# Plain products instead of seven-product ones for the first two query graphs, and another place for a small fold

## The chip, the cores and the metric

The kernel runs on one core of a Trainium2 chip. The metric is the device time of one execution in microseconds (us). Engines are named as in the profile: PE is TensorE, DVE is VectorE, ACT is ScalarE, POOL is GpSimd, SP is the engine that issues the DMAs.

## What is computed

Sixteen graphs of 1024 nodes with 256 channels share one adjacency matrix. Each batch element goes through a graph-weighted attention with a layer norm, and then through two graph convolutions with a layer norm. Cut to what matters:

```python
fea = transpose(x)                                  # B, C, N
c_adj = mean(fea, axis=1)
diff = c_adj[:, None, :] - c_adj[:, :, None]
A = abs(abs(sigmoid(diff) - 0.5) - 0.5) * 2
Wg = adj[None] * (A + A^T) * 0.5
q = relu(einsum('bcn,bnm->bcm', fea, Wg) * para)    # the query graph
k, v = x @ kv_w
x1 = layernorm(x + softmax(q k^T * scale) v)        # 4 heads of 64
h = relu(x1 w1_loop + adj (x1 w1_neigh) + b1)
h = relu(h w2_loop + adj (h w2_neigh) + b2)
out = layernorm(x1 + (x1 + h) * 0.5)
```

The change touches how the query graph q is made: a product of x^T (256 x 1024) with the weighted adjacency matrix Wg (1024 x 1024), different for each batch element.

## The kernel before

All arithmetic is in fp32. A "row" is a tile of 128 x 1024; 21 of them circulate in SBUF and are given out again as their last readers finish. PSUM is divided into three "big" tiles of two banks and two "bank" tiles of one.

The order of all work is written out by hand in `run()`; each engine executes its instructions in that order and waits by semaphores. For each batch element the order is: four attention units (`att.scores(u)`, `att.outputs(u)`; a unit is a pair of heads and half of the nodes), between which the graph convolution of the element before it (`conv.first`, `second`, `last`) is placed; then the query graph of the next element; then its keys and values. `att.add(u)` divides by the softmax denominators (a small PE product with the constant `fold`, L477), adds to x (L487) and sums (L488). `BlockedNorm` is the layer norm after the attention: `mean()` folds these sums on PE (`fold_sums`, L214) and subtracts (L265, L268); `squares()` squares on ACT (L274) and sums on DVE (L275); `variance()` folds again (L214) and takes the power on POOL (L281); `scale()` and `spread()` finish it.

The query graph of an element is prepared in 128-row parts t = 0 to 7. `load(t)` brings a part of adj (L343), `likeness(t)` makes the weight on ACT with Abs and Tanh (L348, L349), `times_adj(t)` multiplies by adj on DVE (L354). From these parts, seven block products in the manner of Strassen and Winograd are made in place of eight: `left` forms four sums of blocks of x on POOL (L361 to L364), `right(k)` four differences of weights on DVE for the parts k and 4 + k (L374 to L377), `step(k)` the seven products on PE (L402), accumulated over k = 0 to 3 in seven PSUM banks (three big tiles and one bank tile), and `end` combines them on DVE with seven additions (L411 to L418), multiplies by `para` (L420) and applies Relu (L421).

Element 0 is special: its query graph comes first of all, beside the loads of all constants. During element 0, when no graph convolution runs yet (`conv` is None), the transposed adjacency matrix is made as well: `adj_blocked(mt)` loads it in 128-byte pieces into rows (L165), `turn_adj` transposes them on DVE (L694). The query graph of element 1 is made in that stretch. From element 2 on every period has the same order.

The helper classes that the change touches are `Queries` (L324 to L422), its callers in `run()` (L669 to L709 for element 0; `second`, L730 to L735; L742 to L763; L767 to L798), and the path L834 to L852, which is executed only where a denominator is out of range and isn't executed here.

Of the kernel before, what the change touches and what calls it, by code (L numbers as in the profile page):

```python
# [18 lines left out]
def kernel(  # L19
# [63 lines left out]
    def big_psum(name):  # L83
        return psum.tile([P, N], F32, tag="big", name=name, bufs=3)
# [239 lines left out]
    class Queries:  # L324

# [5 lines left out]


        def __init__(self, b, xb):
            self.b, self.xb = b, xb
            self.wg, self.adj, self.T, self.T4 = {}, {}, {}, {}

        def load(self, t):
            self.adj[t] = row_tile(f"adj_{self.b}_{t}")
            nc.sync.dma_start(out=self.adj[t], in_=adj[t * P:(t + 1) * P, :])  # L343

        def likeness(self, t):

            wg = row_tile(f"wg_{self.b}_{t}")
            nc.scalar.activation(wg, self.c_row, AF.Abs, bias=self.c_col[:, t:t + 1], scale=-1.0)  # L348
            nc.scalar.activation(wg, wg, AF.Tanh, scale=-0.5)  # L349
            self.wg[t] = wg  # L350

        def times_adj(self, t):
            wg = self.wg[t]
            nc.vector.scalar_tensor_tensor(wg, wg, 1.0, self.adj.pop(t), op0=ALU.add, op1=ALU.mult)  # L354

        def block(self, i, j):
            return self.xb[:, j * TJ:(j + 1) * TJ, ts(i, P)]
# [19 lines left out]
            nc.vector.tensor_sub(t4, hi[:, h0], t12[:, h1])  # L377
            self.T[k] = (t12, t4)

        def weigh(self, k):  # L380
            for t in (k, TJ + k):
                self.load(t)
                self.likeness(t)
                self.times_adj(t)
            self.right(k)

        def step(self, k):
            if k == 0:
                a, b, c = (big_psum(f"g_ps_{self.b}_{i}") for i in range(3))
                h0, h1 = ts(0, FB), ts(1, FB)  # L390
                self.p = {1: a[:, h0], 6: a[:, h1], 7: b[:, h0], 5: b[:, h1], 2: c[:, h0], 3: c[:, h1],
                          4: bank_psum(f"g_ps_{self.b}_3")}
                self.a = a
            lo, hi = self.wg.pop(k), self.wg.pop(TJ + k)
            t12, t4 = self.T.pop(k)
            h0, h1 = ts(0, FB), ts(1, FB)
            terms = {1: (self.block(0, 0), lo[:, h0]), 2: (self.block(0, 1), hi[:, h0]), 3: (self.S[3], hi[:, h1]),
                     4: (self.block(1, 1), t4), 5: (self.S[0], t12[:, h0]), 6: (self.S[1], t12[:, h1]),
                     7: (self.S[2], lo[:, h1])}
            for n in (1, 6, 2, 7, 4, 5, 3):  # L400
                x_n, w_n = terms[n]
                nc.tensor.matmul(self.p[n], x_n[:, k, :], w_n, start=(k == 0), stop=(k == TJ - 1))  # L402

# [258 lines left out]
    def run():  # L662

        xT, c_col = prepare_first(x_first)  # L669
        q = Queries(0, x_first)  # L670
        q.left(nc.gpsimd)
        for k in range(TJ):
            q.load(k)
            q.load(TJ + k)
        load_para()
        blocked = load_blocked(1, "1")
        load_weights()

        def first_weights():
            q.c_row, q.c_col = first_row(c_col), c_col  # L680
            q.likeness(0)

        kT = keys(0, xT, first_weights)
        q.likeness(TJ)
        q.times_adj(0)
        v = values(0, xT, nc.vector.tensor_copy)
        q.times_adj(TJ)
        q.right(0)
        xb = load_x(1, "1")
        tiles = {}  # L690

        def turn_adj(mts):
            for mt in mts:
                nc.vector.transpose(adjT_sb[:, mt, :], tiles.pop(mt))  # L694

        ready = {}
        for k in range(1, TJ):
            for t in (k, TJ + k):
                q.likeness(t)
                q.times_adj(t)  # L700
            q.right(k)
        for k in range(TJ):
            q.step(k)
            if k == 1:
                xB = load_blocked(0, "a0")
                ready["xT"], ready["part"] = prepare(blocked, "1")
            if k == 2:
                ready["mean"] = means(ready["part"], "1")
        qT = q.end()  # L709
        old = conv = None  # L710
        for b in range(B):
            more = b + 1 < B
            att = Attention(b, xB, qT, kT, v)
            if conv and more:
                xb = load_x(b + 1, str(b + 1))

            def first():
                blocked = load_blocked(b + 1, str(b + 1))
                conv.first(blocks=True)
                if old:  # L720
                    old.moments()
                conv.turn_blocks(0)
                ready["xT"], ready["part"] = prepare(blocked, str(b + 1))
                if old:
                    old.finish(out[b - 2])
                conv.turn_blocks(1)
                att.add(0)
                ready["mean"] = means(ready["part"], str(b + 1))

            def second():  # L730
                q.c_row, q.c_col = ready["mean"]
                q.left(nc.gpsimd)
                q.weigh(0)
                conv.second(blocks=True)
                att.add(1)  # L735

            def last():
                conv.last()
                att.add(2)

            between = [first, second, last] if conv and more else []
            if more:  # L742
                q = Queries(b + 1, xb)
            for u in range(len(UNITS)):
                att.scores(u)
                if u == 3 and more:
                    for t in (2, TJ + 2, 3, TJ + 3):
                        q.load(t)
                    for t in (2, TJ + 2, 3, TJ + 3):
                        q.likeness(t)  # L750
                    q.right(1)
                if u and not between:
                    att.add(u - 1)
                att.outputs(u)
                if u == 2 and more:
                    if not conv:
                        q.c_row, q.c_col = ready["mean"]
                        q.left(nc.gpsimd)
                        q.weigh(0)
                    for t in (1, TJ + 1):  # L760
                        q.load(t)
                        q.likeness(t)
                        q.times_adj(t)  # L763
                if u < 3 and between:
                    between[u]()
            norm = BlockedNorm(xB, att.sums, str(b))
            if more:  # L767
                xT = ready["xT"]
                if not conv:
                    for mt in range(4):  # L770
                        tiles[mt] = adj_blocked(mt)

                def pair(k):
                    q.times_adj(k)
                    q.times_adj(TJ + k)
                    q.right(k)

                pair(2)
                q.step(0)
                att.add(3)  # L780
                pair(3)
                q.step(1)
                if not conv:
                    turn_adj(range(4))
                    for mt in range(4, NT):
                        tiles[mt] = adj_blocked(mt)
                norm.mean()
                norm.squares()
                q.step(2)
                q.step(3)  # L790
                qT = q.end()
                xB = load_blocked(b + 1, f"a{b + 1}")
                kT = keys(b + 1, xT, norm.variance)
                norm.scale()
                norm.spread()
                if not conv:
                    turn_adj(range(4, NT))
                v = values(b + 1, xT)  # L798
            else:
                conv.first(lambda: att.add(3))  # L800
                norm.mean()
                norm.squares()
                conv.turn(1)
                conv.neighbours(0)
                norm.variance()
                conv.neighbours(1)
                norm.scale()
                norm.spread()
                conv.last()
                for k, c in ((b - 2, old), (b - 1, conv)):  # L810
                    c.moments()
                    c.finish(out[k])
            old, conv = conv, GraphConv(b, norm.x1, norm.x1T)
        conv.first()
        conv.second()
        conv.ending(out[B - 1])
# [17 lines left out]
    with tc.If(count < P):  # L834
        with tc.For_i(0, B, 1) as b:
# [2 lines left out]
            q = Queries("z", xb)  # L838
            q.c_row, q.c_col = means(part, "z")
            kT, v = keys("z", xT), values("z", xT)  # L840
            q.left(nc.vector)
            for k in range(TJ):
                q.weigh(k)
                q.step(k)
            safe_attention("z", xb, q.end(), kT, v)
            layernorm(xb, "za")
            conv = GraphConv("z", xb, channel_major(blocked_of(xb, "z"), "x1T_z"))
# [34 lines left out]
```

## Time and profile before

| what | value |
|---|---|
| time, median of 3 runs | 2290.58 us (2290.38 to 2290.88) |
| profiled execution, span | 2288.2 us (that run: 2289.93 us) |
| granted PE clock, mean | 0.994 |
| PE products of the query graph (L402) | 896 records, 0.6 us each as shown, 0.43 us from start to start |
| weighted part on ACT (L348 + L349) | 1152 + 1058 ns |
| times adj on DVE (L354) | 1206 ns |
| a difference of weights on DVE (L374 to L377) | 684 to 693 ns |
| an addition at the end (L412 to L418) | 678 to 687 ns |
| times para (L420), Relu (L421) | 1221 ns, 1057 ns |

An fp32 product of 128 x 512 appears as two records of matmul. Records overlap, so the distance from start to start tells what one costs PE. In the lists of waits a row reads: who waited, for whom, us in total, how often, the longest. In a timeline a row reads: start, length, engine, line, operation, tiles, shape, number of instructions, and in brackets the idle time before it and what ended it.

### The profile page before, as it was taken

The page shows a single profiled execution, that of the slowest core. Times are in us where ns is not written, and L with a number is a line of the kernel's source. Part 1 is how long each engine was busy: PE and PEld are TensorE (multiplying, and loading weights), DVE is VectorE, ACT ScalarE, POOL GpSimd, SP SyncE. Part 2 cuts the span into 40 slices and gives each one's busy share as a digit, 9 for nine tenths or more (in the row PEclk, how much of TensorE's full clock was granted, in tenths as well). Part 3 has the DMA queues.
Part 4 walks back from the last instruction along what each step waited for, and adds up shares of the span by engine and source line. Part 5 has one row for each costly group of instructions (what it writes and reads, how often), then busy time and mean ns, then how long its engine had stood idle before and what let it go on. Part 6 is the DMA issues. An engine that isn't in the chain of part 4 may idle for free.

```text
span 2288.2 us, 22626 instructions
## 1 busy us (share of the span) xinstructions
PE 2230.9 (97%) x8294; PEld 1066.4 (47%) x8294; DVE 1806.1 (79%) x2423; ACT 946.4 (41%) x1028; POOL 200.1 (9%) x112
## 2 busy tenths in 40 slices
PE   7989999999999999999999999999999999999997
PEld 4334454444544445454444544445444454444454
DVE  6887878878688797887978778887887968879855
ACT  4633534434354343444344344353443535434420
POOL 1100020010200102001020100102001020010001
PEclk9999999999999999999999999999999999999998
DMA  7195252353423425243261522625235342343102
GB/s 186 37 129 111 60 89 73 66 119 74 83 74 70 115 65 107 78 79 83 60 129 56 92 74 55 129 64 88 70 69 116 74 92 67 75 108 65 37 14 80
DMA packets 568470, 189.39 MB, mean 83 GB/s; under 512 B 487072, under 2 KB 551456, under 8 KB 568352
## 3 DMA queue, kind: packets, MB, share of 16 engines
q1 hardware_dynamic: 568080, 187.35, 38.3%
q8 instruction: 67, 1.10, 0.2%
q14 instruction: 51, 0.42, 0.1%
q10 hardware_dynamic: 272, 0.52, 0.1%
HBM read 146.93 MB, written 40.89 MB: 82 GB/s over the span
## 4 chain that ended last, share of the span: by engine, by line
PE 77%; DVE 20%; issue 1%; DMA 1%; SPq 0%; ACT 0%; DVEq 0%; POOLq 0%; POOL 0%; ACTq 0%
PE s L445 15%; PE av L465 14%; PE h_ps L571 10%; PE u_ps L607 10%; PE g_ps L402 8%; DVE acc L454 6%; PE k_ps L307 5%; PE v_ps L319 5%; PE t_ps L557 3%; PE h_ps L569 2%; PE h_ps L614 2%; PE h_ps L615 2%; DVE wg L354 2%; DVE wg L375 1%; DVE xB_a L487 1%
## 5 line engine op out<-in xcount | busy, mean ns | idle before, releaser
L448 ACT ACTIVATE pr<-s 128x1024 f32<-128x1024 f32 x512 | 476.3, 1053 | 200.7 <-PE s L445 200.5
L454 DVE TENSOR_TENSOR acc<-acc,pr 128x1024 f32<-128x1024 f32 x384 | 472.2, 1230 | 41.4 <-ACT pr L448 0.9
L445 PE MATMUL s<-qT,kT 64*128 64x512 f32 x2048 | 458.9, 598 | 7.2 <-ACT qT L421 6.4
L465 PE MATMUL av<-pr,v 128*64 128x512 f32 x2048 | 453.6, 595 | 0.0
L445 PEld LDWEIGHTS s<-qT,kT 64*128 64x128 f32 x2048 | 191.5, 186 | 234.0 <-ACT pr L448 115.0
L465 PEld LDWEIGHTS av<-pr,v 128*64 128x64 f32 x2048 | 141.4, 137 | 300.0 <-issue 263.0
L281 POOL TENSOR_TENSOR rstd<-rstd,neg_half 128x32 f32<-128x32 f32 x16 | 87.0, 5440 | 1641.8 <-DVE rstd L279 1641.8
L571 PE MATMUL h_ps<-adjT_sb,t 128*128 128x512 f32 x512 | 224.9, 592 | 0.0
L607 PE MATMUL u_ps<-adjT_sb,h 128*128 128x512 f32 x512 | 224.5, 596 | 0.1
L348 ACT ACTIVATE wg<-c_row,c_col 128x1024 f32<-128x1024 f32 x128 | 147.5, 1152 | 114.4 <-DVE accB L456 112.4
L607 PEld LDWEIGHTS u_ps<-adjT_sb,h 128*128 128x128 f32 x512 | 95.8, 190 | 126.3 <-issue 125.2
L571 PEld LDWEIGHTS h_ps<-adjT_sb,t 128*128 128x128 f32 x512 | 97.3, 190 | 122.5 <-issue 118.6
L354 DVE SCALAR_TENSOR_TENSOR wg<-wg,adj 128x1024 f32<-128x1024 f32 x128 | 149.3, 1206 | 4.6 <-ACT wg L349 4.6
L349 ACT ACTIVATE wg<-wg 128x1024 f32<-128x1024 f32 x128 | 135.5, 1058 | 4.1
L402 PE MATMUL g_ps<-wg,x 128*128 128x512 f32 x256 | 134.9, 608 | 0.0
L402 PE MATMUL g_ps<-T,S 128*128 128x512 f32 x256 | 131.7, 596 | 3.1 <-DVE T L376 3.1
L402 PE MATMUL g_ps<-wg,S 128*128 128x512 f32 x256 | 131.5, 595 | 0.0
L572 ACT ACTIVATE h1T<-h_ps,b_sb 128x512 f32<-128x512 f32 x32 | 22.0, 687 | 247.7 <-PE h_ps L571 247.7
L307 PE MATMUL k_ps<-xT,kvw_sb 128*128 128x512 f32 x256 | 117.1, 600 | 1.1 <-DVE U L412 1.1
L609 ACT COPY uT<-u_ps 128x512 f32<-128x512 f32 x32 | 18.7, 585 | 228.8 <-PE u_ps L607 228.8
L319 PE MATMUL v_ps<-kvw_sb,xT 128*128 128x256 f32 x512 | 113.1, 379 | 0.0
L580 DVE STREAM_TRANSPOSE h1B<-h1T 128x512 f32<-128x512 f32 x28 | 19.9, 712 | 117.0 <-ACT h1T L572 117.0
(123 smaller groups left out, 2456.1 us busy)
## 6 DMA issues: line engine op xcount, KB each, us to landing
adj<-in_adj_dram SPq DMA_DIRECT2D x128, 512.0 KB, 4.1
xB_a<-in_x_dram SPq DMA_DIRECT2D x128, 128.0 KB, 4.1
x1d<-xB_a SPq DMA_DIRECT2D x128, 128.0 KB, 3.4
x<-x1d SPq DMA_DIRECT2D x16, 1024.0 KB, 5.7
xB<-in_x_dram SPq DMA_DIRECT2D x120, 128.0 KB, 4.5
x<-in_x_dram SPq DMA_DIRECT2D x15, 1024.0 KB, 8.9
out_dram<-x SPq DMA_DIRECT2D x15, 1024.0 KB, 4.7
h1d<-h1B SPq DMA_DIRECT2D x112, 64.0 KB, 2.2
```

The source lines that it names most:

```text
L307: nc.tensor.matmul(pk[:, ts(j, FB)], kvw_sb[:, cc, ts(kb, P)], xT[:, cc, ts(j, FB)], start=(cc == 0), stop=(cc == NC - 1))
L319: nc.tensor.matmul(pv[:, ts(i, C)], xT[:, cc, ts(g * per + i, P)], kvw_sb[:, cc, C:2 * C], start=(cc == 0), stop=(cc == NC - 1))
L348: nc.scalar.activation(wg, self.c_row, AF.Abs, bias=self.c_col[:, t:t + 1], scale=-1.0)
L349: nc.scalar.activation(wg, wg, AF.Tanh, scale=-0.5)
L354: nc.vector.scalar_tensor_tensor(wg, wg, 1.0, self.adj.pop(t), op0=ALU.add, op1=ALU.mult)
L402: nc.tensor.matmul(self.p[n], x_n[:, k, :], w_n, start=(k == 0), stop=(k == TJ - 1))
L445: nc.tensor.matmul(ps[:, ts(s, FB)], self.kT[rows, pair, ts(mt, P)], self.qT[rows, pair, ts(j, FB)], start=True, stop=True)
L448: nc.scalar.activation(pr, ps, AF.Exp)
L454: nc.vector.tensor_add(acc, acc, pr)
L465: nc.tensor.matmul(pav[s * HD:(s + 1) * HD, :], self.v[:, mt, pair * P + s * HD:pair * P + (s + 1) * HD], self.pr[mt][:, ts(s, FB)], start ...
L571: nc.tensor.matmul(ph, t1[:, mt, :], adjT_sb[:, mt, ts(j, FB)], start=False, stop=(mt == NT - 1))
L607: nc.tensor.matmul(pu, self.h1[:, ts(mt, P)], adjT_sb[:, mt, ts(j, FB)], start=(mt == 0), stop=(mt == NT - 1))
```

## The change

The class `Queries` becomes the plain form: `step(t)` for t = 0 to 7 multiplies one 128-row part, four products each (two blocks of channels, two halves of the nodes), accumulated in two big PSUM tiles; `end` multiplies by `para` straight out of PSUM. The seven-product form becomes the class `FastQueries`, used for elements 2 to 15. Elements 0 and 1 (and the path that isn't executed) use the plain form, and their surroundings in `run()` are written anew. In the seven-product form the first three steps take their products in another order, and the norm's `mean()` and `squares()` are issued inside the third step, ahead of its product 7, instead of ahead of that step.

```diff
     class Queries:
         def __init__(self, b, xb):
             self.b, self.xb = b, xb
-            self.wg, self.adj, self.T, self.T4 = {}, {}, {}, {}
+            self.wg, self.adj = {}, {}
+            self.pg = None
...
+        def weigh(self, t):
+            self.likeness(t)
+            self.times_adj(t)
...
+        def step(self, t):
+            if t == 0:
+                self.pg = [big_psum(f"g_ps_{self.b}_{cb}") for cb in range(NC)]
+            wg = self.wg.pop(t)
+            for cb in range(NC):
+                for j in range(NJ):
+                    nc.tensor.matmul(self.pg[cb][:, ts(j, FB)], self.xb[:, t, ts(cb, P)], wg[:, ts(j, FB)],
+                                     start=(t == 0), stop=(t == NT - 1))
+
+        def end(self):
+            qT = work.tile([P, NC, N], F32, tag="qT", name=f"qT_{self.b}")
+            for cb in range(NC):
+                nc.vector.tensor_mul(qT[:, cb, :], self.pg[cb], para_sb[:, cb, :])
+                nc.scalar.activation(qT[:, cb, :], qT[:, cb, :], AF.Relu, scale=QSCALE)
+            return qT
+
+    class FastQueries(Queries):
...
-        def weigh(self, k):
-            for t in (k, TJ + k):
-                self.load(t)
-                self.likeness(t)
-                self.times_adj(t)
+        def pair(self, k):
+            self.times_adj(k)
+            self.times_adj(TJ + k)
             self.right(k)
-        def step(self, k):
+        def step(self, k, halfway=None):
...
-            for n in (1, 6, 2, 7, 4, 5, 3):
+            for n in (1, 6, 2, 7, 4, 5, 3) if k == TJ - 1 else (1, 2, 3, 5, 7, 6, 4):
+                if n == 7 and halfway:
+                    halfway()
...
         q = Queries(0, x_first)
-        q.left(nc.gpsimd)
-        for k in range(TJ):
-            q.load(k)
-            q.load(TJ + k)
+        for t in range(NT):
+            q.load(t)
...
             q.c_row, q.c_col = first_row(c_col), c_col
-            q.likeness(0)
+            q.weigh(0)
         kT = keys(0, xT, first_weights)
-        q.likeness(TJ)
-        q.times_adj(0)
+        for t in (1, 2):
+            q.likeness(t)
         v = values(0, xT, nc.vector.tensor_copy)
-        q.times_adj(TJ)
-        q.right(0)
+        for t in (1, 2):
+            q.times_adj(t)
...
-        for k in range(1, TJ):
-            for t in (k, TJ + k):
-                q.likeness(t)
-                q.times_adj(t)
-            q.right(k)
-        for k in range(TJ):
-            q.step(k)
-            if k == 1:
+        for t in range(NT):
+            if t + 3 < NT:
+                q.weigh(t + 3)
+            q.step(t)
+            if t == 4:
                 xB = load_blocked(0, "a0")
                 ready["xT"], ready["part"] = prepare(blocked, "1")
-            if k == 2:
+            if t == 6:
                 ready["mean"] = means(ready["part"], "1")
...
             def second():
                 q.left(nc.gpsimd)
-                q.weigh(0)
+                for t in (0, TJ):
+                    q.load(t)
+                    q.likeness(t)
+                q.pair(0)
...
-                q = Queries(b + 1, xb)
+                q = (FastQueries if conv else Queries)(b + 1, xb)
...
                 if u == 2 and more:
-                    if not conv:
+                    if conv:
+                        for t in (1, TJ + 1):
+                            q.load(t)
+                            q.likeness(t)
+                            q.times_adj(t)
+                    else:
                         q.c_row, q.c_col = ready["mean"]
-                        q.left(nc.gpsimd)
-                        q.weigh(0)
-                    for t in (1, TJ + 1):
-                        q.load(t)
-                        q.likeness(t)
-                        q.times_adj(t)
+                        for t in range(3):
+                            q.load(t)
+                            q.weigh(t)
...
+            if more and not conv:
+                for t in range(3, NT):
+                    q.load(t)
+                for t in range(3, NT):
+                    q.likeness(t)
+                for mt in range(4):
+                    tiles[mt] = adj_blocked(mt)
+                q.times_adj(3)
+                q.step(0)
+                q.times_adj(4)
+                q.step(1)
+                att.add(3)
+                turn_adj(range(4))
+                for mt in range(4, NT):
+                    tiles[mt] = adj_blocked(mt)
+                q.times_adj(5)
+                q.step(2)
+                q.step(3)
+                norm.mean()
+                q.times_adj(6)
+                q.times_adj(7)
+                q.step(4)
+                norm.squares()
+                q.step(5)
+                q.step(6)
+                norm.variance()
+                xB = load_blocked(b + 1, f"a{b + 1}")
+                q.step(7)
+                qT = q.end()
+                norm.scale()
+                norm.spread()
+                turn_adj(range(4, NT))
+                kT, v = keys(b + 1, xT), values(b + 1, xT)
+            elif more:
-                pair(2)
+                q.pair(2)
                 q.step(0)
                 att.add(3)
-                pair(3)
+                q.pair(3)
                 q.step(1)
-                norm.mean()
-                norm.squares()
-                q.step(2)
+                q.step(2, lambda: (norm.mean(), norm.squares()))
                 q.step(3)
```

More of the change, by code (lines that the diff above doesn't have):

```diff
@@ L354, in times_adj, with __init__ @@
             nc.vector.scalar_tensor_tensor(wg, wg, 1.0, self.adj.pop(t), op0=ALU.add, op1=ALU.mult)
+        def step(self, t):
[13 more added lines that the diff above has]
+    class FastQueries(Queries):
+        def __init__(self, b, xb):
+            super().__init__(b, xb)
+            self.T = {}
         def block(self, i, j):
@@ L392, in step @@
                           4: bank_psum(f"g_ps_{self.b}_3")}
-                self.a = a
             lo, hi = self.wg.pop(k), self.wg.pop(TJ + k)
@@ L694, in turn_adj @@
                 nc.vector.transpose(adjT_sb[:, mt, :], tiles.pop(mt))
-        ready = {}
-        for k in range(1, TJ):
-            for t in (k, TJ + k):
-                q.likeness(t)
-                q.times_adj(t)
-            q.right(k)
-        for k in range(TJ):
-            q.step(k)
-            if k == 1:
+        for t in range(NT):
[3 more added lines that the diff above has]
+            if t == 4:
                 xB = load_blocked(0, "a0")
+                ready = {}
                 ready["xT"], ready["part"] = prepare(blocked, "1")
-            if k == 2:
+            if t == 6:
                 ready["mean"] = means(ready["part"], "1")
@@ L742, in run @@
             if more:
-                q = Queries(b + 1, xb)
+                q = (FastQueries if conv else Queries)(b + 1, xb)
             for u in range(len(UNITS)):
                 att.scores(u)
-                if u == 3 and more:
+                if u == 3 and more and conv:
                     for t in (2, TJ + 2, 3, TJ + 3):
@@ L766, in run @@
             norm = BlockedNorm(xB, att.sums, str(b))
-            if more:
+            if more and not conv:
                 xT = ready["xT"]
[L769 to L776, printed above, removed]
-                pair(2)
+                for t in range(3, NT):
[31 more added lines that the diff above has]
+            elif more:
+                xT = ready["xT"]
+                q.pair(2)
                 q.step(0)
                 att.add(3)
-                pair(3)
+                q.pair(3)
                 q.step(1)
[L783 to L786, printed above, removed]
-                norm.mean()
-                norm.squares()
-                q.step(2)
+                q.step(2, lambda: (norm.mean(), norm.squares()))
                 q.step(3)
@@ L795, in run @@
                 norm.spread()
-                if not conv:
-                    turn_adj(range(4, NT))
                 v = values(b + 1, xT)
@@ L840 @@
             kT, v = keys("z", xT), values("z", xT)
[L841 to L844, printed above, removed]
+            for t in range(NT):
+                q.load(t)
+                q.weigh(t)
+                q.step(t)
             safe_attention("z", xb, q.end(), kT, v)
```

## The prediction

> **What bounds the kernel now.** I read the page first.
>
> ```profile
> PE 2230.9 (97%) x8294; PEld 1066.4 (47%) x8294; DVE 1806.1 (79%) x2423; ACT 946.4 (41%) x1028; POOL 200.1 (9%) x112
> ...
> PE 77%; DVE 20%; issue 1%; DMA 1%; SPq 0%; ACT 0%; DVEq 0%; POOLq 0%; POOL 0%; ACTq 0%
> ```
>
> PE is busy for 97% of the span: what counts is the work put on PE and the few waits left in it. The view of waits, cut to PE:
>
> ```profile
> PE sum_ps L214 <- DVE sums L488: 14.8, 14, 1.1
> PE g_ps L402 <- DVE den_max L483: 9.1, 1, 9.1
> PE s L445 <- ACT qT L421: 6.4, 1, 6.4
> ...
> PE g_ps L402 <- DVE T L376: 3.1, 1, 3.1
> PE mean_ps L214 <- DVE part L207: 2.6, 2, 2.0
> PE k_ps L307 <- DVE U L412: 1.1, 1, 1.1
> ```
>
> The first recurs 14 times, once for each batch whose queries are made from batch 2 on. The others happen once each, in the first 160 us. Third, the timeline around the recurring wait, and its one occurrence without a wait (145.94, ahead of batch 1):
>
> ```profile
> 145.94 0.53 PE L214 MATMUL sum_ps<-sums,fold 128*128 128x32 f32 x4
> 146.30 1.10 PE L402 MATMUL g_ps<-wg,x 128*128 128x512 f32 x2
> ...
> 285.78 0.30 PE L214 MATMUL sum_ps<-sums,fold 128*128 128x32 f32 x2
> 287.15 0.41 PE L214 MATMUL sum_ps<-sums,fold 128*128 128x32 f32 x2 [1.06 <-DVE sums L488]
> 287.39 1.10 PE L402 MATMUL g_ps<-wg,x 128*128 128x512 f32 x2
> 291.93 0.18 DVE L265 TENSOR_SCALAR mean<-sum_ps 128x32 f32<-128x32 f32 x1
> ```
>
> From the fold's first record to the next product takes 1.61 us with the wait and 0.36 without: 1.25 us per batch. VectorE reads the result only at 291.93, 4.5 us later. Last, the windows where the granted clock (eighth figure, ahead of the DMA share) is down:
>
> ```profile
> 55.00:60.00 5.00, 0.18 (x1) 0.00 (x0) 4.68 (x7) 0.00 (x0) 0.00 (x0) 0.77 0.00 0
> 60.00:65.00 5.00, 3.46 (x10) 1.68 (x12) 1.53 (x2) 3.14 (x3) 0.00 (x0) 0.55 0.00 0
> ...
> 130.00:135.00 5.00, 0.52 (x1) 0.50 (x2) 4.88 (x10) 4.94 (x5) 0.00 (x0) 0.50 1.33 154
> 135.00:140.00 5.00, 5.00 (x9) 1.98 (x8) 4.90 (x8) 3.35 (x4) 0.00 (x0) 0.54 1.46 130
> ```
>
> In both places PE was idle for over 6 us while VectorE was full, and then ran at half speed for some us.
>
> **What the skill says.** "TensorE: Matmul & The Clock Gate", section "What's actually happening": the clock gate falls to half after an idle window of about 3.4 us and opens after about as long a busy one. The trace agrees: 0.50 to 0.55 in these windows, 1.00 in the windows around them. "PSUM — Partial Sum Buffer", "Specifications": eight banks of 2 KiB. The kernel gives six to three "big" tiles and two to "bank" tiles, so the seven products' seventh bank is taken from the denominators; the 9.1 us wait on den_max is that. "VectorE: DVE Perf Modes", "Why PSUM operands drop a tier": an fp32 operation that reads PSUM stays at the basic rate. The trace has 0.68 us for 128x512 with a PSUM operand (L414) and 0.69 us without (L374): no penalty, so I price the product that reads PSUM over 1024 columns like L420, at 1.22 us. "DMA: Bandwidth & Descriptors", "Specifications": line rate wants 512 B or more. The 128-byte loads of adjB land about 1.0 us apart for 128 KB each, the plain adj loads 1.28 us apart for 512 KB: the trace agrees.
>
> **The change, part by part**, on the profiled span of 2288.2 us (that run took 2289.93; the three timed runs had 2290.38 to 2290.88). An fp32 product shows as two records of 0.43 us: 896 records at L402 are 16 batches of 28 products, 0.86 us each.
>
> *Added PE work.* Plain: 8 steps x 4 products = 32 instead of 28, so 4 x 0.86 = 3.4 us per batch, 6.9 us for two. All of it is on PE's path.
>
> *Removed.* In each of the two batches: 16 subtractions of 0.69 us (11.0 us of VectorE), seven additions of 0.68 us (4.8), a ScalarE copy (0.57) and four POOL operations of 1.3 us. Off PE's path except where PE waits for them, which the next two paragraphs follow.
>
> *Batch 0.* PE still reaches the first product at 24.18. VectorE is free of the copies of v at 25.1, then needs 1.2 us per weighted tile; ScalarE makes one in 2.13 us, the last at 33.3. Step t needs its tile at 24.2 + 3.43t: step 1 wants it at 27.6 and has it at 26.3, step 7 at 48.6 against 34.5. So the 3.1 us wait goes. On SP the eight loads of adj only change order (all land by 17.8, para and the rest behind them keep their places). The two S rows are not taken, so the blocked load of x behind them no longer waits for a row. Transposes and sums of batch 1's x (4.7 us of VectorE) end near 39, long before the fold for the mean at 48.2: the 2.6 us wait goes. PE ends step 7 at 52.0. The first half of the result is complete 1.7 us earlier; VectorE comes from the mean (1.9 us, to 50.7), multiplies (1.22), ScalarE relu (1.06): scores start at 53.1 instead of 61.54, after 1.1 us of idle, too short for the clock to fall. That is 8.4 us, plus 1.5 for the cold start (the first 32 records of L445 took 8.61 us, later ones 7.14), less about 0.4 because the second relu stands ahead of the first exp: 9.5 us.
>
> *Between.* At 109.60 PE waited 1.0 us for exps that stood behind four likenesses (8.5 us of ScalarE). Now there are three (6.4): gone. The first step of batch 1 starts near 110.9 instead of 121.66.
>
> *Batch 1.* Plain sums use two big tiles and no bank: the 9.1 us wait and the cold records after it (about 2.8 us) go. New waits come from VectorE. Shifting the old rows: partial denominators of unit 3 at 116.2, add(2) to 119.0, o to 119.7, times_adj(3) 120.9, (4) 122.1, add(3) 124.9, four transposes of adj to 129.5, times_adj(5) 130.7, mean and subtraction 133.2, times_adj(6) and (7) 134.4 and 135.6, squares 138.0. PE: steps 0 and 1 to 117.8, denominators, step 2 to 121.5, step 3 to 125.0, fold at 125.0 to 125.4 (wait 0.1), step 4 to 128.8, step 5 waits 2.0 for times_adj(5), step 6 waits 0.3, the second fold 0.2, step 7 ends at 141.9; keys and values need 14.1 as before. Batch 1's scores start at 156.0 instead of 174.13: 18.1 us. The four transposes need adjB by 127.2: SP now has five adj loads ahead, and two of the four tiles get rows that unit 3 frees near 116; eight transfers at 1.0 us from there land at 126. A close fit.
>
> Check from the other side: PE's lost time ahead of 174 us is 3.2 + 3.0 + 6.5 + 1.4 + 1.0 + 9.3 + 2.8 + 1.3 = 28.5 (start-to-start excess, cold records included); less 6.9 of work and some 4.5 of new waits, 17.1. I take 17.6. Bounds: 21.6 if no new wait appears, 10 if a late adjB costs 4 us and a cold clock 3 more.
>
> *The fold inside the third step, 14 batches.* Products 1, 2, 3, 5 (3.43 us) now stand between the end of step 1 (285.78) and the fold, so the sums (ready at 287.0) are 2.2 us early at 289.2. Behind the fold in PE's queue are products 7, 6, 4, which wait for nothing new: T of step 2 is complete at 284.3. Step 3 then starts at 292.2; its product 6 at 293.1 needs T from 291.3. The mean's result is there at 289.6 and VectorE takes it at 291.9 as before, so nothing of the chain subtract, square, reduce moves. The keys now want the bank of products 1 and 6 at 298.2; VectorE frees it with L412 at 297.5: 0.7 us of margin instead of 2.0. The new order in steps 0 to 2 costs nothing: same count, and PE did not wait for T there in these batches. Gain 14 x 1.25 = 17.5 us; bounds 14.8 (the idle that the waits view counts) and 18.3 (14 x 1.31, the fold's own start-to-start excess). In q.pair(0) times_adj(0) moves behind the second likeness; per-engine orders stay, no cost.
>
> Sum: 17.6 + 17.5 = 35.1 us; 2290.6 - 35.1 = 2255.5.
>
> **Rivals.** (A, 0.72) As worked: 2255.5, own range 2250 to 2261. (B, 0.15) VectorE or the adjB transfers hold the plain steps of batch 1: if all four adjB tiles wait for unit 3's rows, the last lands near 134, times_adj(5) to (7) follow 6 to 7 us later, and PE loses that and up to 3 us of clock. Gain 17.6 - 8 = 9.6 there; 2263. For it: DMA at 1.3 to 1.6 of its share in those 30 us; against: earlier start of all loads. (C, 0.07) The recurring wait returns as a wait of the keys for L412, whose margin shrinks to 0.7 us: with VectorE 1.3 us later than I think, half to all of the 17.5 is lost: 2264 to 2273. Against: no row of that chain depends on PE's place. (D, 0.05, the other side) The same place, one step worse: the mean's chain (fold, subtraction, square, reduce, L412) starts later because the fold is 3.43 us further back in PE's queue. It makes the kernel slower once L412 slips by over 0.7 + 35.1/14 = 3.2 us in each batch; at 4.5 us: 14 x 3.8 - 35.1 = 18 us slower, 2309. Against: VectorE is occupied with step 3's weights until 291.9. That the change does nothing (0.01) is excluded by the count of products.
>
> **Numbers.** Faster by over 0.2% (4.6 us, about what a measurement of this kernel can tell from none): A, B and C, less 0.01 for a case where B and C meet: 0.93; within 0.2%: that 0.01 and the 0.01 of no effect, 0.02; slower: D, 0.05. The range 2250 to 2264 holds A, most of B and the edge of C.
>
> **What would show it.** Right: no PE wait of sum_ps for sums in the steady batches and a period of 138.4 instead of 139.7 us (287.15 to 426.83 now); clock 1.00 from 20 to 200 us; scores of batch 0 near 53 and of batch 1 near 156; 64 plain products, 128 records, in place of 112. Wrong: a wait of k_ps for L412 in every batch, PE waiting for wg or adj beyond 3 us between 110 and 142, or scores of batch 1 later than 164.

## The result and the profile after

The kernel after takes 2253.19 us (median; 2252.71 to 2253.66) against 2290.76 us (2290.38 to 2291.44) for the kernel before on the same chip: a ratio of 0.9836, interval 0.9823 to 0.9848, 37.6 us less. The forecast was 2255.5, range 2250 to 2264. The profiled span is 2251.1 us, 37.1 less than before. A batch, below, is one of the sixteen elements; a period is the time from the first scores of one batch to those of the next.

The page of the kernel after, the same two lines as shown of before:

```profile
PE 2230.0 (99%) x8310; PEld 1067.2 (47%) x8310; DVE 1773.9 (79%) x2377; ACT 945.4 (42%) x1026; POOL 187.6 (8%) x104
...
PE 98%; DVE 1%; DMA 0%; ACT 0%; issue 0%; SPq 0%; POOLq 0%; DVEq 0%; POOL 0%; ACTq 0%
```

PE's busy time has hardly changed (2230.9 before), though 16 records were added, 6.9 us by the prediction's count: in part because records that the low clock had made longer are gone (1.5 + 2.8 us by the same count); the rest was not followed up. VectorE's part of the chain that ended last falls from 20% to 1%. A part of 20% did not mean 20% to gain: the chain had passed through VectorE's work in each batch because of a wait of about 1 us at its end.

PE's waits, kernel after (who, for whom, us, times, longest):

```profile
PE xT_ps L185 <- DMA x<-in_x_dram: 4.9, 2, 4.8
PE g_ps L357 <- DVE wg L349: 1.1, 1, 1.1
PE s L473 <- ACT qT L364: 0.7, 1, 0.7
PE h1n_ps L620 <- ACT h1T L600: 0.3, 1, 0.3
```

Of the six waits shown of before none is left at its size. The first here is the arrival of x at the start, which was there before too (5.0 us). The third is the old wait of 6.4 us for the first query tile.

The first two batches, timeline of the kernel after:

```profile
23.91 24.20 PE L357 MATMUL g_ps<-wg,x 128*128 128x512 f32 x56
48.30 3.68 PE L357 MATMUL g_ps<-wg,x 128*128 128x512 f32 x8
52.67 7.42 PE L473 MATMUL s<-qT,kT 64*128 64x512 f32 x32 [0.69 <-ACT qT L364]
...
129.55 7.33 PE L357 MATMUL g_ps<-wg,x 128*128 128x512 f32 x16 [1.14 <-DVE wg L349]
140.59 7.03 PE L307 MATMUL k_ps<-xT,kvw_sb 128*128 128x512 f32 x16
```

Seven plain steps run without a gap. The scores of batch 0 start at 52.67 instead of 61.54. One new wait stands at step 5 of batch 1. The scores of batch 1 start at 154.46 instead of 174.13: 19.7 us of the gain lie here. The windows in which the clock had been down, kernel after (eighth figure: granted clock):

```profile
55.00:60.00 5.00, 5.00 (x24) 1.51 (x20) 3.60 (x3) 5.00 (x7) 0.00 (x0) 1.00 0.00 0
60.00:65.00 5.00, 5.00 (x26) 1.78 (x26) 4.58 (x5) 1.65 (x2) 0.00 (x0) 1.00 0.00 0
...
130.00:135.00 5.00, 5.00 (x13) 2.01 (x11) 5.00 (x5) 2.11 (x2) 0.00 (x0) 1.00 0.96 138
135.00:140.00 5.00, 5.00 (x16) 2.54 (x15) 2.63 (x4) 0.00 (x0) 2.37 (x1) 1.00 1.10 146
```

A later batch, timeline of the kernel after around the fold:

```profile
266.75 0.69 DVE L516 TENSOR_REDUCE sums<-xB_a 128x16 f32<-128x512 f32 x1
...
269.56 0.53 PE L214 MATMUL sum_ps<-sums,fold 128*128 128x32 f32 x4
...
272.28 0.18 DVE L265 TENSOR_SCALAR mean<-sum_ps 128x32 f32<-128x32 f32 x1
...
277.17 0.68 DVE L440 TENSOR_TENSOR U<-P,g_ps 128x512 f32<-128x512 f32 x1
...
278.59 3.60 PE L307 MATMUL k_ps<-xT,kvw_sb 128*128 128x512 f32 x8
```

The fold takes its four records in one go, with no wait, after the sums have been there for 2.1 us. VectorE takes the mean 2.7 us after it. L440 (L412 of before) ends 0.7 us ahead of the keys that want its bank. From scores to scores a later batch takes 138.44 us instead of 139.68; 14 such periods give 17.4 us. 19.7 + 17.4 = 37.1, the whole difference of the spans.

### The profile page after: what moved, and what is told of

Its sections match the earlier page's. It is cut to its first block, busy times and chain, and to the rows that moved or that the text cites. A ratio compares the mean times of both kernels' runs of the same rounds, so it can differ in the third digit from the quotient of the medians.

```text
span 2251.1 us, 22596 instructions
## 1 busy us (share of the span) xinstructions
PE 2230.0 (99%) x8310; PEld 1067.2 (47%) x8310; DVE 1773.9 (79%) x2377; ACT 945.4 (42%) x1026; POOL 187.6 (8%) x104
## 4 chain that ended last, share of the span: by engine, by line
PE 98%; DVE 1%; DMA 0%; ACT 0%; issue 0%; SPq 0%; POOLq 0%; DVEq 0%; POOL 0%; ACTq 0%
PE s L473 20%; PE av L493 20%; PE g_ps L430 15%; PE h_ps L599 10%; PE u_ps L635 10%; PE k_ps L307 5%; PE v_ps L319 5%; PE t_ps L585 3%; PE h_ps L597 2%; PE h_ps L642 2%; PE h_ps L643 2%; PE g_ps L357 2%; PE den_ps L505 1%; PE sum_ps L214 1%; PE mean_ps L214 0%; DMA x<-in_x_dram 0%
## 5 line engine op out<-in xcount | busy, mean ns | idle before, releaser
L430 PE MATMUL g_ps<-wg,S 128*128 128x512 f32 x224 | 115.5, 597 | 0.0
L430 PE MATMUL g_ps<-T,S 128*128 128x512 f32 x224 | 114.4, 592 | 0.0
L430 PE MATMUL g_ps<-wg,x 128*128 128x512 f32 x224 | 110.2, 604 | 0.0
```

## The experiments

Theory: PE is the bound, so its time is its products plus its waits; each wait that goes returns in full and each product costs in full. Rivals: the new order of the products, not the fold's place, brings the gain of the later batches; the relief of VectorE in batches 0 and 1 carries on into them; and the slower case of the prediction, in which a fold too far back holds the keys. Each kernel keeps the whole computation. Times are compared with the kernel before run on the same chip, 2290.7 to 2291.3 us.

**The later part alone**, on the kernel before:

```diff
-            for n in (1, 6, 2, 7, 4, 5, 3):
+            for n in (1, 6, 2, 7, 4, 5, 3) if k == TJ - 1 else (1, 2, 3, 5, 7, 6, 4):
+                if n == 7 and halfway:
+                    halfway()
...
-                norm.mean()
-                norm.squares()
-                q.step(2)
+                if conv:
+                    q.step(2, lambda: (norm.mean(), norm.squares()))
+                else:
+                    norm.mean()
+                    norm.squares()
+                    q.step(2)
```

> The kernel before, with only the later part of the change: new order of the seven products in the first three steps, and mean and squares inside the third step from batch 2 on. My theory (PE's waits and products add up, the two halves of the change are independent): period 138.44 instead of 139.68 us, 14 x 1.24 = 17.4 us less, 2273.4. The rival that VectorE, relieved in batches 0 and 1, is what makes the sums come in time: 2290 to 2291.

Measured: 2275.76 us, ratio 0.9933 (0.9917 to 0.995). The period is 138.44 us in every later batch, so the rival of VectorE's relief falls: the fold's new place needs nothing from batches 0 and 1. But the time is 2.4 us over the forecast. The timeline of PE in batch 0 of this kernel shows where:

```profile
26.31 1.13 PE L404 MATMUL g_ps<-wg,x 128*128 128x512 f32 x2 [1.06 <-DVE wg L354]
...
47.82 0.60 PE L214 MATMUL mean_ps<-part,fold 128*128 128x32 f32 x2 [4.08 <-DVE part L207]
...
49.31 2.06 PE L404 MATMUL g_ps<-wg,x 128*128 128x512 f32 x2
51.15 1.91 PE L404 MATMUL g_ps<-T,S 128*128 128x512 f32 x2
```

The kernel before, the same view, waits 3.1 us at 28.28 and 2.0 us at 47.65:

```profile
28.28 1.10 PE L402 MATMUL g_ps<-T,S 128*128 128x512 f32 x2 [3.08 <-DVE T L376]
...
47.65 0.38 PE L214 MATMUL mean_ps<-part,fold 128*128 128x32 f32 x2 [1.96 <-DVE part L207]
```

The new order shortens the first wait by 2.0 us, but VectorE has the sums for the mean at 47.7 and 47.8 in the two kernels, so PE only arrives there earlier and idles 4.1 us in one piece. The clock falls to half at 47.5 for 6.8 us, and the next products take twice as long. Scores of batch 0 start at 64.41 instead of 61.54. Whether that reading holds was tried by itself: **the later part alone, with the old order in batches 0 and 1.** The edit against the run above:

```diff
-            for n in (1, 6, 2, 7, 4, 5, 3) if k == TJ - 1 else (1, 2, 3, 5, 7, 6, 4):
+            for n in (1, 6, 2, 7, 4, 5, 3) if k == TJ - 1 or self.b in (0, 1) else (1, 2, 3, 5, 7, 6, 4):
```

> The kernel before with only the later part of the change, as in the first experiment, but batches 0 and 1 keep the old order of products. My reading of the first experiment: the new order in batch 0 turns two waits (3.1 and 2.0 us) into a short one and one of 4.1 us, in which the clock falls. With the old order scores of batch 0 are back at 61.5 instead of 64.4, no half clock near 47, and 14 x 1.24 = 17.4 us less than before remain: 2273.5. If the new order had no part in it: 2275.8 again.

Measured: 2273.49 us, ratio 0.9924 (0.9908 to 0.9941); scores of batch 0 at 61.60, no low clock near 47. A low stretch of 3.4 us at 28.4 stands behind the 3.1 us wait, where the kernel before has none; it did not move the scores (last section). The reading holds, and 17.4 us is the worth of the later part.

**The plain queries alone**, on the kernel after:

```diff
-            for n in (1, 6, 2, 7, 4, 5, 3) if k == TJ - 1 else (1, 2, 3, 5, 7, 6, 4):
+            for n in (1, 6, 2, 7, 4, 5, 3):
...
-                q.step(2, lambda: (norm.mean(), norm.squares()))
+                norm.mean()
+                norm.squares()
+                q.step(2)
```

> The kernel after, with the fold back ahead of the third step and the old order of products: only the plain queries of batches 0 and 1 are left of the change. My theory: batch 1's scores at 154.5 as after, period 139.68 as before, 14 x 1.24 = 17.4 us more than after, 2270.6. The rival that the relief of VectorE carries on into the later batches: a period under 139.5 and a time near 2253 to 2260.

Measured: 2269.98 us, ratio 0.9911 (0.9894 to 0.9927), period 139.68. PE's waits in this kernel hold the old line again:

```profile
PE sum_ps L214 <- DVE sums L516: 14.8, 14, 1.1
```

The two parts together, 17.4 and 21.2 us against the runs beside them, are the 37.6 us of the whole within the intervals (3 to 4 us each side): no interaction shows.

**The fold's place, in five steps.** All on the kernel after; the edit moves the point at which `mean()` and `squares()` are issued. First the old order of products with the fold still ahead of product 7:

```diff
-            for n in (1, 6, 2, 7, 4, 5, 3) if k == TJ - 1 else (1, 2, 3, 5, 7, 6, 4):
+            for n in (1, 6, 2, 7, 4, 5, 3):
                 if n == 7 and halfway:
```

> The kernel after, with the old order 1, 6, 2, 7, 4, 5, 3 in all four steps. The fold stays ahead of product 7, now behind three products of the third step (2.6 us) instead of four (3.4). My theory: 2.6 us is more than the wait of 1.25, so period 138.44 and 2253.2, no change. The rival that the order of the products brings the gain of the later batches: period back at 139.68, 2270.6.

Measured: 2253.06 us, ratio 0.9836 (0.982 to 0.9852), period 138.44. The order of the products brings nothing to the later batches; the rival falls. Then the fold behind one product only:

```diff
-                if n == 7 and halfway:
+                if n == 2 and halfway:
```

> The kernel after, with mean and squares ahead of product 2 of the third step, so that only one product (0.86 us) stands ahead of the fold. My theory: 0.86 of the 1.24 us is covered and about 0.39 us of waiting for the sums returns in each of 14 batches: period 138.83, 2258.6. If the gain were all or nothing (the wait drops out by the change of place itself): 2253.2 or 2270.6.

Measured: 2258.34 us, ratio 0.9858 (0.9842 to 0.9875), period 138.83. The timeline of PE in this kernel:

```profile
266.47 0.30 PE L214 MATMUL sum_ps<-sums,fold 128*128 128x32 f32 x2
266.97 0.41 PE L214 MATMUL sum_ps<-sums,fold 128*128 128x32 f32 x2 [0.20 <-DVE sums L516]
```

The wait shrinks by the time of the product put ahead of it and not more. Third, the fold between the third and the fourth step:

```diff
-                q.step(2, lambda: (norm.mean(), norm.squares()))
+                q.step(2)
+                norm.mean()
+                norm.squares()
```

> The kernel after, with mean and squares between the third and the fourth step, 2.6 us later than after. My theory: VectorE takes the mean 2.7 us after the fold in the kernel after (269.56 and 272.28), so it is delayed by at most 0.5 us, and the keys' bank (free 0.7 us before it is wanted) still comes in time: period 138.44, 2253.2. If VectorE's chain were already the limit there: 14 x 0.4 = 6 us more, 2259.

Measured: 2252.64 us, ratio 0.9833 (0.9818 to 0.9848), period 138.43: there is room of at least 2.6 us behind the place chosen. Fourth, three products into the fourth step:

```diff
-                q.step(2, lambda: (norm.mean(), norm.squares()))
-                q.step(3)
+                q.step(2)
+                q.step(3, lambda: (norm.mean(), norm.squares()))
```

> The kernel after, with mean and squares ahead of product 7 of the fourth step, 5.2 us later than after. My theory, the price of the slower rival of the prediction: the mean is taken at 275.2 instead of 272.28, L440 ends 2.9 us later at 280.7, the keys want its bank at 278.6, so PE waits 2.1 to 2.4 us for L440 in each of 14 batches: period 140.6 to 140.8, 2283 to 2287. If the keys did not depend on that chain: 2253.2.

Measured: 2298.44 us, ratio 1.0034 (1.002 to 1.0047): slower than the kernel before, and 11 us slower than the theory allowed. The predicted wait is there; PE's waits and VectorE's timeline of this kernel:

```profile
PE k_ps L307 <- DVE U L440: 30.1, 14, 2.1
```

```profile
416.15 0.19 DVE L265 TENSOR_SCALAR mean<-sum_ps 128x32 f32<-128x32 f32 x1 [2.92 <-PE sum_ps L214]
...
421.05 0.68 DVE L440 TENSOR_TENSOR U<-P,g_ps 128x512 f32<-128x512 f32 x1
```

What was not counted is the clock. The periods alternate between 140.85 us (138.44 + 2.41, as worked out) and 142.54. The windows around the keys of two batches that follow each other (second figure: PE's busy time; eighth: granted clock). They are cut where the second batch's low stretch begins, at 422.84, and whole steps of 3.413 us, its length, from there:

```profile
276.07:279.48 3.41, 2.71 (x7) 0.93 (x5) 3.36 (x4) 2.56 (x3) 0.00 (x0) 1.00 0.00 0
279.48:282.89 3.41, 1.96 (x5) 1.00 (x6) 3.38 (x6) 0.03 (x1) 0.00 (x0) 1.00 0.00 0
282.89:286.31 3.42, 3.42 (x13) 1.75 (x12) 3.35 (x5) 0.31 (x1) 0.00 (x0) 1.00 0.00 0
...
419.43:422.84 3.41, 1.26 (x4) 0.58 (x4) 3.41 (x5) 0.92 (x2) 0.00 (x0) 1.00 0.00 0
422.84:426.25 3.41, 3.41 (x6) 1.35 (x5) 3.31 (x6) 0.00 (x0) 0.00 (x0) 0.50 0.00 0
426.25:429.66 3.41, 3.41 (x13) 1.74 (x12) 1.80 (x3) 2.73 (x3) 1.53 (x1) 1.00 0.00 0
```

After the same idle of 2.15 us the clock stays up in one batch and falls to half for 3.4 us in the next: seven falls, 1.7 us each, make the missing 11.8 us. In the first batch the idle is split over two steps (0.70 and 1.45 us), in the second it lies in one; the last section returns to this. Fifth, one product earlier in that step, to see whether a shorter idle spares the clock (the edit against the fourth):

```diff
-                if n == 7 and halfway:
+                if n == 2 and halfway:
```

> The kernel after, with mean and squares behind two products of the fourth step instead of three as in the sixth experiment. There the keys waited 2.3 us per batch and the clock fell in every second batch. One product less: the wait is 0.86 us shorter, 1.45 to 1.55 us. If the clock stays up at that length: period 139.9 to 140.0 in every batch, 2274 to 2275. If it still falls in every second batch: 12 us more, 2286.

Measured: 2274.75 us, ratio 0.993 (0.9914 to 0.9947), period 139.99 in every batch. PE waits 1.3 us for L440 in each of 14 batches and the clock stays up. One product of 0.86 us between the two places is worth 23.7 us of time: 12 for the wait itself and 12 for the clock.

**Plain queries in all batches**, on the kernel after:

```diff
+    class PlainPairs(Queries):
...
+        def pair(self, k):
+            self.times_adj(k)
+            self.times_adj(TJ + k)
+        def step(self, k, halfway=None):
+            super().step(k)
+            if halfway:
+                halfway()
+            super().step(TJ + k)
...
-                q = (FastQueries if conv else Queries)(b + 1, xb)
+                q = (PlainPairs if conv else Queries)(b + 1, xb)
```

> The kernel after, with plain queries in all batches: the parts of adj come in the order 0, 4, 1, 5, 2, 6, 3, 7, eight steps of four products, no sums of x and no differences of weights. My theory: PE has no wait left in the later batches, so the four added products count in full, 14 x 3.43 = 48 us more, period 141.87, 2301.2. If the relief of VectorE (15.8 us per batch) gave PE something back there: less than 2295.

Measured: 2299.14 us, ratio 1.0035 (1.0021 to 1.0048), period 141.74: 3.30 us more per batch. PE's timeline of this kernel:

```profile
395.79 7.13 PE L357 MATMUL g_ps<-wg,x 128*128 128x512 f32 x16
402.76 0.30 PE L522 MATMUL den_ps<-den_part,fold 128*128 128x32 f32 x2
402.90 10.55 PE L357 MATMUL g_ps<-wg,x 128*128 128x512 f32 x24
413.29 0.53 PE L214 MATMUL sum_ps<-sums,fold 128*128 128x32 f32 x4
413.65 10.55 PE L357 MATMUL g_ps<-wg,x 128*128 128x512 f32 x24
424.04 2.31 PE L307 MATMUL k_ps<-xT,kvw_sb 128*128 128x512 f32 x5
```

From the first product to the keys it takes 28.25 us, against 24.94 in the kernel after (392.09 to 417.03). The products account for 3.4 of it; 0.1 comes back at the denominators, which follow the products after 0.14 us here and 0.25 there. VectorE's 15.8 us less per batch give PE nothing else: where PE has no waits, the plain form is the dearer one.

**One of the first two batches at a time**, on the kernel after: the queries of batch 1 by seven products in the surroundings of the kernel before, with the old order of products,

```diff
-                q = (FastQueries if conv else Queries)(b + 1, xb)
+                q = FastQueries(b + 1, xb)
...
-                        for t in range(3):
-                            q.load(t)
-                            q.weigh(t)
+                        q.left(nc.gpsimd)
+                        q.weigh_both(0)
```

> The kernel after, but batch 1's queries by seven products in the order and surroundings of the kernel before; batch 0 stays plain. My theory: scores of batch 0 at 52.7, no cold start there (10.4 us together), the 9.1 us wait of batch 1 for a bank and its cold records are back: 9.3 us more than after, 2262.5. If VectorE's lead from batch 0 (no sums on POOL beside it, an earlier start) shortens that wait as well: down to 2259.

and those of batch 0:

```diff
-        q = Queries(0, x_first)
-        for t in range(NT):
-            q.load(t)
+        q = FastQueries(0, x_first)
+        q.left(nc.gpsimd)
+        for k in range(TJ):
+            q.load(k)
+            q.load(TJ + k)
```

> The kernel after, but batch 0's queries by seven products as in the kernel before; batch 1 stays plain. My theory: scores of batch 0 at 61.5 and cold until 64.5, the rest as after: 10.4 us more than after, 2263.6. If part of batch 1's gain needs batch 0's: more than 2265.

Measured: 2262.95 us, ratio 0.9876 (0.9859 to 0.9892), and 2265.25 us, ratio 0.9886 (0.9869 to 0.9902). With batch 1 by seven products, the old wait for a bank stands in PE's timeline at its old length, though batch 0 is plain:

```profile
124.36 2.07 PE L437 MATMUL g_ps<-T,x 128*128 128x512 f32 x2 [9.03 <-DVE den_max L518]
```

With batch 0 by seven products its scores start at 61.67, and those of batch 1 at 164.82, 10.36 us later than in the kernel after; 10.4 were forecast. That the second kernel is 1.7 us over the forecast lies for 0.7 us in two of its later periods, which are 0.35 us longer than the others (why was not followed up); the other 1.0 us does not show in this trace, whose execution took 2264.15 us, 1.1 less than the median. Against the kernel after, by the traces up to batch 1's scores, the seven products of batch 0 cost 10.4 us (12.1 by the times) and those of batch 1 9.6 from scores to scores (9.8 by the times).

In each of these two batches the edit puts back the form and the old order of work around it together. The plain form needs no "bank" tile, so with it no product can wait for one; whether seven products with another order of VectorE's work would also have lost that wait was not tried.

**A next step: the last wait of batch 1**, on the kernel after:

```diff
                 att.add(3)
+                for t in range(5, NT):
+                    q.times_adj(t)
                 turn_adj(range(4))
...
-                q.times_adj(5)
-                q.times_adj(6)
-                q.times_adj(7)
...
-                norm.variance()
                 xB = load_blocked(b + 1, f"a{b + 1}")
                 q.step(7)
+                norm.variance()
```

> The kernel after, with the last three weighted parts of batch 1 made ahead of the four transposes of adj, and step 7 ahead of the second fold. My theory: the last wait of PE in that stretch (1.3 us at 129.55, step 5 for the weighted part 5) goes and no other takes its place, batch 1's scores at 153.2 instead of 154.46, 2251.9; too little for the times to tell, the timeline tells. If the mean's chain, 1.2 us later, holds PE at the second fold: 2253.2.

Measured: 2251.74 us, ratio 0.9828 (0.9814 to 0.9841). The times don't tell it from the kernel after (0.9823 to 0.9848). PE's timeline does:

```profile
125.05 13.98 PE L357 MATMUL g_ps<-wg,x 128*128 128x512 f32 x32
```

All 16 products from step 4 on run in one piece; from the scores of batch 0 to those of batch 1 it takes 100.18 us instead of 101.79.

## Why the prediction was right

*The later batches.* Forecast 14 x 1.25 = 17.5 us; measured 14 x 1.24 = 17.4. Each step of the argument holds: one product ahead of the fold covers 0.86 us of the wait, three or more all of it, and the order of the products does nothing. The margin of 0.7 us at L412 was read rightly: it is 0.7 us in the kernel after.

*Batch 0.* Scores forecast at 53.1, measured at 52.67, with the 3.1, 2.6 and 6.4 us waits and the cold start gone as described; the idle of 1.1 us that was forecast is 0.7.

*Batch 1.* Scores forecast at 156.0, measured at 154.46. The bank wait and its cold records went. The fit of the adjB transfers held: VectorE turned four tiles from 123.8 to 128.4 without a break. The term that was mis-sized is the new waits: 2.0 + 0.3 + 0.2 + 0.1 = 2.6 us forecast, from start to start 1.3 measured at step 5 (1.1 in the list of waits) and some 0.1 at step 6, since VectorE ran some 1.2 us ahead of the shifted rows (times_adj(5) ended at 129.5, not 130.7). PE also reached the first step 0.6 us earlier than forecast (110.31, not 110.9). Two sums gave 18.1 and 17.1 us for the first two batches, and a value between them was taken; the trace has 19.7. The sum from the other side had the same fault: with the waits that were measured, 0.7 for the first query tile and 1.3 at step 5, in place of its 4.5, it gives 28.5 - 6.9 - 2.0 = 19.6. So the new waits account for most of the 2.3 us by which the forecast was high.

*The rivals.* B (adjB or VectorE holding batch 1) did not occur. C and D described a real edge: two places further back for the fold cost what their margin says, and the farther one makes the kernel slower than before. They did not happen because the place chosen lies 2.6 us or more short of that edge; the two costs put it at 2.7 us, an estimate (five products, 4.29 us later, cost 1.55 a batch; six, 5.15 later, 2.41). D's price was too low: it counted the wait of the keys and left out the clock, which adds a third to it.

## What to carry to other kernels

Where one engine is busy for 97% of the span, list its waits by how often they come. A wait of one microsecond that recurs in every period can be filled by moving it behind work that is ready, as far as the first consumer of its result allows; read both margins, ahead and behind, before choosing the place. An algorithm with fewer products on the bound engine paid here only where the helper engine kept up with its work for it: seven products won 3.3 us per batch in the steady periods and, in the old order of work, lost some 10 in each of the first two, where PE waited for VectorE. A wait removed ahead of another wait may only lengthen the second.

## What had not been expected

The clock. In the kernel before it was low after idles of over 6 us. The runs narrow that down: an idle of 1.3 us left it up in 14 of 14 cases, one of 2.15 us brought it down for 3.4 us in 7 of 14, in every second batch, and one of 4.1 us for 6.8 us. The wait of 3.1 us in batch 0 left it up in the kernel before, and brought it down for 3.4 us in the later part with the old order and for 6.8 us with batch 0 alone back at seven products. So the length of an idle alone does not decide.

The Trainium skill ("TensorE: Matmul & The Clock Gate", section "What's actually happening") gives a window of about 3.4 us that runs freely, and lets the clock fall after one idle window, as the prediction took it. The traces agree with the free-running window: up to the end of the work the low stretches last 3.41 us or two to four times that, and within a trace they start whole multiples of 3.413 us apart (in the kernel with the fold three products into the fourth step 283.31 us each, 83.0 steps). They don't agree that a whole window must be idle. With these steps laid over PE's records of all fourteen traces, a step at full clock with at most 1.95 us of idle was followed by one at full clock, and one with 2.09 us or more by one at half. The seven idles of 2.15 us that brought the clock down lie in one step each, the other seven are split by a boundary; of the 3.1 us wait, at most 1.80 us fell in one step in the kernel before, 3.08 and 2.25 in the two kernels where the clock fell. This is a reading of traces that lie beside each other; no run moved an idle against the steps on purpose. It fits every fall of the clock on record here, with limits found for these kernels alone.
